# A deformable convolution on TensorE: strips of two rows in place of four, and more distance between the engines

## The chip, the cores and the metric

The kernel runs on one core of a Trainium2 chip. The metric is the device time of one execution in microseconds (us), taken as the median of three runs. Beside it stands one execution under the hardware profiler, which has a time of its own.

## The reference

Two layers in float32 on an image batch `x` of shape (2, 256, 128, 128), each a residual block that begins with a group norm over 32 groups (`_gn`). Layer 0 is a deformable 3x3 convolution: two plain 3x3 convolutions of the normalised input give, for each pixel and each of the 9 taps, an offset and a mask; the input is sampled bilinearly at the shifted place; the samples go through the weights.

```python
def _L0_conv_ref(x, w_conv, b_conv, w_off, b_off, w_mask, b_mask):
    offset = _conv2d(x, w_off, b_off)
    mask = jax.nn.sigmoid(_conv2d(x, w_mask, b_mask))
    ...
    py = base_y[None] + dy
    px = base_x[None] + dx
    sampled = jax.vmap(_deform_sample)(x, py, px)
    sampled = sampled * mask[:, None]
    out = jnp.einsum('bckhw,ock->bohw', sampled, w_conv.reshape(COUT, C, K2))
    return out + b_conv[None, :, None, None]
...
x = x + _L0_conv_ref(_gn(x), ...)
x = x + _L1_conv_ref(_gn(x), ...)
```

Layer 1 sends the normalised image through eight low-rank experts (a 1x3 convolution to 8 channels, a 3x1 convolution back to 256) and adds their outputs with the weights `probs`.

## The kernel before

**Stages.** At first (about 170 us) the kernel reads image 0, takes its statistics, and writes a table to DRAM: for every pixel one entry of 4 KB to be fetched, holding the four neighbours' 256 channels (four corners of 1 KB). Then comes the stream, which fills most of the time: all samples of image 0, then those of image 1. Beside image 0's samples the table of image 1 is built; beside image 1's samples layer 1 of image 0 runs. At the end (from about 3990 us) layer 1 of image 1 runs alone.

**A unit.** The stream's smallest step is a unit: one tap `k` of one image row `r`, that is 128 pixels, one to a partition. There are 2 x 128 x 9 = 2304 units. A unit passes through five engines:

- `gather` (L567, POOL): an indirect DMA fetches 128 entries of 4 KB into a tile `g`.
- `product` (L577, ACT): the first corner times its weight makes the accumulator `acc`.
- `add` (L583, DVE), three times: the other corners, times their weights, are added to `acc`.
- `turn` (L593, PE): two transposes of 128x128 put the sampled row, channels now on the partitions, into a PSUM tile `ptr` that takes two rows.
- `keep` (L601, ACT): each pair of rows is copied from `ptr` to an SBUF tile `sm`.
- `apply_tap` (L608, PE): the tap's weights times `sm`, accumulated over 9 taps and two halves of the input channels in a PSUM bank `po`.

After the ninth tap `residual` (L617, DVE) adds `po`, the bias and the old `x` into the tile of `x`, `result_stats` (L621) takes statistics for the next norm, and `store_x1` writes the rows out where they don't stay in SBUF.

**Chunks.** The order of units is: chunks of four rows (`CR`), in a chunk the nine taps, in a tap the four rows. So `sm` holds four rows (512 columns), and each of the four units of a tap issues one matmul of 512 columns: two output halves `m` times two input halves `h`. The halves `m` have a PSUM bank each, both used by every chunk.

**Order.** The instructions are issued in an order written out by hand, by a loop over slots `s`, one unit to a slot. Every engine works off its instructions in that order; semaphores keep the data dependencies. In slot `s` the loop issues the gather of unit `s + GA`, the product of `s + LP`, adds of `s + 1` and `s`, the tap of `s - LM`, the transposes of `s - TL`, and for every second unit the copy of `s - TL - KL`:

```python
if when(s + GA):
    gather(s + GA)
if when(s + LP):
    product(s + LP)
...
if when(s - TL):
    turn(s - TL)
if when(s - TL - KL) and (s - TL - KL) % 2 == 1:
    keep(s - TL - KL)
for piece in sched.pop(s, ()):
    piece()
```

All other work (offsets of the next group of rows, loads of `x`, the table of image 1, layer 1, residuals) hangs in `sched`, at slots given by `put`. How far one engine may run ahead of another follows from these distances and from the number of buffers: 15 tiles `g`, 8 `acc`, 3 `sm`, 3 `ptr`.

PSUM has eight banks: three for `ptr`, three (`p_m`) for all side work, two for `po`.

Of the kernel before, what the change touches and what calls it, by code (L numbers as in the profile page):

```python
# [32 lines left out]
F32 = mybir.dt.float32  # L33
# [6 lines left out]
P = 128  # L40
# [18 lines left out]
ER = 64  # L59
ROUND = 12582912.0  # L60

UPC = K2 * CR
UPG = UPC * CPG
UPI = UPG * NG
UNITS = B * UPI
GA = 15
LP = 3
TL = 1
KL = 2
LM = 8  # L70
XB, XR = 3, 5


@with_exitstack
def layers(ctx, tc, x, w_om, b_om, w_cv, b_cv, w_in, w_out, probs, out):
# [444 lines left out]


    gp = pool(stream, "gather", GA)
    ap = pool(stream, "acc", 8)
    sp = pool(stream, "sampled", 3)
    st = pool(stream, "stat", 1)
    p_o = pool(stream, "p_o", 1, space=PSUM)
    p_t = pool(stream, "p_t", 3, space=PSUM)
    oc = pool(stream, "offs", 1)
    pieces, _, last_rows = offset_pieces(0, oc, p_m, "m")
# [19 lines left out]

    def unit(u):  # L550
        b, u = divmod(u, UPI)
        ci, u = divmod(u, UPC)
        k, r = divmod(u, CR)
        return b, ci, k, r

    gts, accs, pts, sms, pos_, stats1 = {}, {}, {}, {}, {}, {}

    def sample_of(u):
        b, ci, k, r = unit(u)
        idx, wt = ready[b, ci // CPG]  # L560
        return idx, wt, (ci % CPG) * CR + r, k

    def gather(u):
        b, ci, k, r = unit(u)
        idx, _, rr, k = sample_of(u)
        gt = gp.tile([P, 2 * CELL], F32, tag="gt", name=f"g_{b}_{ci}_{k}_{r}")
        nc.gpsimd.indirect_dma_start(  # L567
            out=gt[:], out_offset=None, in_=tables[b][:, :],
            in_offset=bass.IndirectOffsetOnAxis(ap=idx[:, rr, k : k + 1], axis=0),
        )  # L570
        gts[u] = gt

    def product(u):
        b, ci, k, r = unit(u)
        _, wt, rr, k = sample_of(u)
        acc = ap.tile([P, C], F32, tag="acc", name=f"acc_{b}_{ci}_{k}_{r}")
        nc.scalar.activation(acc, gts[u][:, 0:C], AF.Copy, scale=wt[:, 0, rr, k : k + 1])  # L577
        accs[u] = acc

# [5 lines left out]
        )  # L585

    def turn(u):
        b, ci, k, r = unit(u)
        if r % 2 == 0:
            pts[u // 2] = p_t.tile([P, NH, 2 * W], F32, tag="t", name=f"ptr_{b}_{ci}_{k}_{r}")  # L590
        acc = accs.pop(u)
        for h in range(NH):
            nc.tensor.transpose(  # L593
                pts[u // 2][:, h, (r % 2) * W : (r % 2 + 1) * W], acc[:, h * P : (h + 1) * P], ident
            )

    def keep(u):
        b, ci, k, r = unit(u)
        if r == 1:
            sms[u // CR] = sp.tile([P, NH, N], F32, tag="sm", name=f"sm_{b}_{ci}_{k}")  # L600
        nc.scalar.copy(sms[u // CR][:, :, (r - 1) * W : (r + 1) * W], pts.pop(u // 2))  # L601

    def apply_tap(u):
        b, ci, k, i = unit(u)
        m, h = divmod(i, NH)
        if k == 0 and h == 0:
            pos_[b, ci, m] = p_o.tile([P, N], F32, tag=f"o{m}", name=f"po_{b}_{ci}_{m}")
        nc.tensor.matmul(  # L608
            pos_[b, ci, m], lhsT=wcv[:, h, k, m * P : (m + 1) * P], rhs=sms[u // CR][:, h],
            start=(k == 0 and h == 0), stop=(k == K2 - 1 and h == NH - 1),  # L610
        )

    def residual(b, ci, m):
        xt = xts[b, ci // CPG]
        at_ = (ci % CPG) * N
        v = xt[:, m, at_ : at_ + N]
        nc.vector.scalar_tensor_tensor(v, pos_.pop((b, ci, m)), bcv[:, m : m + 1], v, ALU.add, ALU.add)  # L617

    def result_stats(b, ci, m):
        at_ = (ci % CPG) * N  # L620
# [6 lines left out]
    def table_beside(b):  # L627
# [57 lines left out]
        for j in range(NCH):  # L685
            g, i = divmod(j, CPG)
            if g < NG - XR:
                put(slot, lambda j=j: load(j, "xs"))
            elif i == 0:

                slot = max(slot, UPG * (g - NG + XR + 1) + LM + 12)
# [222 lines left out]
    assert tabled < UPI - GA - 16  # L914
    put(UPI - 16, sides.close)
    put(UPI, lambda: result_stats_of(1))
    slot = UPI + LM + 10
# [18 lines left out]
    while s < end or any(t >= s for t in sched):  # L936
# [21 lines left out]
        if when(s - TL - KL) and (s - TL - KL) % 2 == 1:  # L958
# [69 lines left out]
```

## Time and profile before

| | us |
|---|---|
| median of 3 runs | 4062.48 |
| lowest, highest | 4056.1, 4065.21 |
| profiled execution: time | 4155.75 |
| profiled execution: span from first to last instruction | 4154.0 |

| engine | busy us | share of the span |
|---|---|---|
| PE, matmuls | 3497.9 | 84% |
| PE, weight loads | 1870.3 | 45% |
| DVE | 3442.1 | 83% |
| ACT | 1837.6 | 44% |
| POOL | 2335.4 | 56% |

The profiled execution is 93 us longer than the median of the runs, so sums made from the profile are made against 4155.75 us. A row of the profile names a source line, an engine, an operation, its tiles (out<-in), how often it came, its busy time and the mean of one; then the idle time of the engine just before these instructions, and what ended it. A wait names the waiting instruction, the one that ended the wait, the total, how often, and the longest; "remote" there means that the profile doesn't tell what ended it, "issue" that the engine waited for nothing that the profile shows. Matmuls are pipelined and their ends modelled, so a mean of one is longer than the distance from one to the next.

### The profile page before, as it was taken

The page shows a single profiled execution, that of the slowest core. Times are in us where ns is not written, and L with a number is a line of the kernel's source. Part 1 is how long each engine was busy: PE and PEld are TensorE (multiplying, and loading weights), DVE is VectorE, ACT ScalarE, POOL GpSimd, SP SyncE. Part 2 cuts the span into 40 slices and gives each one's busy share as a digit, 9 for nine tenths or more (in the row PEclk, how much of TensorE's full clock was granted, in tenths as well). Part 3 has the DMA queues.
Part 4 walks back from the last instruction along what each step waited for, and adds up shares of the span by engine and source line. Part 5 has one row for each costly group of instructions (what it writes and reads, how often), then busy time and mean ns, then how long its engine had stood idle before and what let it go on. Part 6 is the DMA issues. An engine that isn't in the chain of part 4 may idle for free.

```text
span 4154.0 us, 51837 instructions
## 1 busy us (share of the span) xinstructions
PE 3497.9 (84%) x14044; PEld 1870.3 (45%) x14044; DVE 3442.1 (83%) x8066; ACT 1837.6 (44%) x3883; POOL 2335.4 (56%) x2388
## 2 busy tenths in 40 slices
PE   3588888888878888888889888889988889888889
PEld 2443434444444444444444444444545445444444
DVE  6488988888888887889788888888888888888887
ACT  2244444445444554444444444444444444444432
POOL 0356666656665666656566555556656556555531
PEclk9699999999999999989999999999999999999999
DMA  9999999999999999999889999999999999988835
GB/s 360 358 358 370 356 371 346 342 335 366 372 372 378 389 394 387 376 361 369 315 329 349 333 344 345 334 350 340 363 339 356 331 349 354 351 320 327 327 118 193
DMA packets 419516, 1425.46 MB, mean 343 GB/s; under 512 B 41582, under 2 KB 45338, under 8 KB 419098
## 3 DMA queue, kind: packets, MB, share of 16 engines
q0 software_dynamic: 331776, 1208.11, 78.0%
q1 hardware_dynamic: 87450, 214.04, 13.6%
q8 instruction: 114, 1.87, 0.2%
q14 instruction: 176, 1.44, 0.1%
HBM read 1298.20 MB, written 123.78 MB: 342 GB/s over the span
## 4 chain that ended last, share of the span: by engine, by line
PE 42%; DVE 25%; DMA 12%; issue 11%; another core or an unknown queue 6%; ACT 3%; POOL 1%; POOLq 1%; SPq 0%; ACTq 0%; DVEq 0%
PE po L608 23%; DVE acc L583 19%; DMA g<-table,cidx 9%; PE ptr L593 7%; PE pu L335 3%; PE pe L832 2%; PE ph L766 2%; DMA table<-hpx 2%; ACT acc L577 1%; PE ph L811 1%; PE pe L847 1%; DVE stats L621 1%; POOL g L567 1%; DVE x L617 1%
## 5 line engine op out<-in xcount | busy, mean ns | idle before, releaser
L583 DVE SCALAR_TENSOR_TENSOR acc<-g,wt,acc 128x256 f32<-128x256 f32 x6912 | 2961.8, 480 | 466.3 <-ACT acc L577 325.7
L567 POOL DMA_INDIRECT g<-table,cidx x2304 | 2284.5, 992 | 1530.9 <-DVE acc L583 556.5
L608 PE MATMUL po<-sm,wcv 128*128 128x512 f32 x4608 | 2502.1, 625 | 301.5 <-ACT sm L601 130.8
L601 ACT COPY sm<-ptr 128x512 f32<-128x512 f32 x1152 | 672.7, 584 | 1933.6 <-PE ptr L593 1096.3
L593 PEld LDWEIGHTS ptr<-idp,acc 128*128 128x128 f32 x4608 | 626.4, 146 | 1622.3 <-issue 1075.9
L593 PE MATMUL ptr<-idp,acc 128*128 128x128 f32 x4608 | 935.2, 286 | 195.4 <-ACT sm L601 76.3
L577 ACT ACTIVATE acc<-g,wt 128x256 f32<-128x256 f32 x2304 | 1060.1, 506 | 43.2 <-DMA g<-table,cidx 29.7
L608 PEld LDWEIGHTS po<-sm,wcv 128*128 128x128 f32 x4608 | 753.4, 199 | 375.3 <-ACT sm L601 160.4
L335 PE MATMUL pu<-wus,x 128*128 128x81 f32 (+2 forms) x1448 | 270.1, 313 | 7.8 <-issue 6.7
L335 PEld LDWEIGHTS pu<-wus,x 128*128 128x128 f32 x1448 | 216.8, 200 | 10.3 <-issue 6.9
L617 DVE SCALAR_TENSOR_TENSOR x<-po,bcv,x 128x512 f32<-128x512 f32 x116 | 86.3, 744 | 59.6 <-PE ptr L593 21.8
L832 PE MATMUL pe<-h,wout 128*128 128x256 f32 (+1 forms) x384 | 127.2, 461 | 1.0 <-DVE xc L856 1.0
L766 PE MATMUL ph<-xcn,win 128*64 128x254 f32 (+1 forms) x768 | 98.1, 403 | 4.6 <-issue 4.6
L856 DVE TENSOR_TENSOR xc<-pe,xc 128x512 f32<-128x512 f32 x76 | 49.8, 683 | 44.3 <-PE pe L847 20.0
L350 PE MATMUL om<-u,idp 128*128 128x216 f32 x192 | 56.0, 375 | 33.1 <-ACT u L344 30.7
L832 PEld LDWEIGHTS pe<-h,wout 128*128 128x128 f32 x384 | 67.9, 193 | 33.7 <-issue 30.1
L621 DVE BATCH_NORM_STATS2 stats<-x 128x6 f32<-128x512 f32 x116 | 79.2, 683 | 0.1
L766 PEld LDWEIGHTS ph<-xcn,win 128*64 128x64 f32 x768 | 55.9, 145 | 37.6 <-issue 16.6
L847 PE MATMUL pe<-h,wout 64*128 64x128 f32 (+1 forms) x752 | 70.1, 322 | 1.3 <-issue 1.3
L504 DVE COPY hpx<-hpt 128x512 f32<-128x512 f32 x32 | 21.1, 687 | 57.2 <-DMA table<-hpx 47.0
L799 DVE TENSOR_TENSOR v<-xcn 128x512 f32<-128x512 f32 x96 | 65.9, 744 | 1.8 <-ACT xcn L786 1.8
L847 PEld LDWEIGHTS pe<-h,wout 64*128 64x128 f32 x752 | 52.1, 187 | 27.4 <-issue 18.8
(115 smaller groups left out, 1019.3 us busy)
## 6 DMA issues: line engine op xcount, KB each, us to landing
g<-table,cidx POOLq DMA_INDIRECT x2304
table<-tpx SPq DMA_DIRECT2D x32, 1024.0 KB
table<-hpx SPq DMA_DIRECT2D x15, 2048.0 KB
x<-in_x_dram SPq DMA_DIRECT2D x29, 1024.0 KB
out_dram<-xc SPq DMA_DIRECT2D x38, 512.0 KB
x<-x SPq DMA_DIRECT2D x16, 1024.0 KB
out_dram<-x SPq DMA_DIRECT2D x26, 512.0 KB
xs<-in_x_dram SPq DMA_DIRECT2D x22, 512.0 KB
```

The costliest lines, as they stand in the source:

```text
L335: nc.tensor.matmul(held["ps", j][:, lo:hi], lhsT=xt[:, h, r * W : (r + 1) * W], rhs=w[:, lo - i + 2 : hi - i + 2], start=(i == 2 and h == ...
L567: nc.gpsimd.indirect_dma_start(out=gt[:], out_offset=None, in_=tables[b][:, :], in_offset=bass.IndirectOffsetOnAxis(ap=idx[:, rr, k : k + ...
L577: nc.scalar.activation(acc, gts[u][:, 0:C], AF.Copy, scale=wt[:, 0, rr, k : k + 1])
L583: nc.vector.scalar_tensor_tensor(accs[u], gt[:, q * C : (q + 1) * C], wt[:, q, rr, k : k + 1], accs[u], ALU.mult, ALU.add)
L593: nc.tensor.transpose(pts[u // 2][:, h, (r % 2) * W : (r % 2 + 1) * W], acc[:, h * P : (h + 1) * P], ident)
L601: nc.scalar.copy(sms[u // CR][:, :, (r - 1) * W : (r + 1) * W], pts.pop(u // 2))
L608: nc.tensor.matmul(pos_[b, ci, m], lhsT=wcv[:, h, k, m * P : (m + 1) * P], rhs=sms[u // CR][:, h], start=(k == 0 and h == 0), stop=(k == K ...
L617: nc.vector.scalar_tensor_tensor(v, pos_.pop((b, ci, m)), bcv[:, m : m + 1], v, ALU.add, ALU.add)
L621: nc.vector.bn_stats(stats1[b][:, m, ci], xts[b, ci // CPG][:, m, at_ : at_ + N])
L766: nc.tensor.matmul(o[:, :, to], lhsT=win[:, h, tap], rhs=pairs[:, t, :, of], start=(q == 0), stop=(q == 5),)
L832: nc.tensor.matmul(ps[t][:, m], lhsT=wout[:, 2 * t, m * P : (m + 1) * P], rhs=hs[ci], start=(banks or m == 0), stop=False,)
L847: nc.tensor.matmul(ps[t][:, m, to], lhsT=wout[half, 1, m * P : (m + 1) * P], rhs=hs[c][half, of], start=False, stop=(banks or m == NH - 1) ...
```

## The change

- Chunks become strips of two rows (`SR`): in a strip the nine taps, in a tap two rows. `sm` holds two rows (256 columns) and has four buffers. Each of the two units of a tap issues two matmuls of 256 columns, for one output half `m` and both input halves `h`.
- Both output halves of a strip share one PSUM bank, and the pool of `po` has two buffers, which the strips use in turn. Only the strip's first matmul carries `start`.
- `residual` works on 256 columns, once for each half of each strip, and is issued `LR` = 6 slots after the strip's last tap (before: 2). `result_stats` is still taken once for four rows and half, two slots after the residual; the store follows.
- `LP`: the first product is issued 6 units ahead, not 3. `KL`: the copies stand 4 slots behind the transposes, not 2. There are 15 buffers `acc`, not 8.
- `GA`: 14 buffers for gathers, 14 units ahead, not 15.
- Loads of `x` for the next group are issued 52 slots ahead, not 54; two other due slots are written in terms of `LR`, the one for layer 1 of image 0 falling two slots later.

```diff
-UPC = K2 * CR
-UPG = UPC * CPG
+SR = 2
+SPC = CR // SR
+SPG = GR // SR
+UPS = K2 * SR
+UPG = UPS * SPG
...
-GA = 15
-LP = 3
+GA = 14
+LP = 6
 TL = 1
-KL = 2
+KL = 4
 LM = 8
+LR = 6
...
-    ap = pool(stream, "acc", 8)
-    sp = pool(stream, "sampled", 3)
+    ap = pool(stream, "acc", 15)
+    sp = pool(stream, "sampled", 4)
     st = pool(stream, "stat", 1)
-    p_o = pool(stream, "p_o", 1, space=PSUM)
+    p_o = pool(stream, "p_o", 2, space=PSUM)
...
     def keep(u):
-        b, ci, k, r = unit(u)
-        if r == 1:
-            sms[u // CR] = sp.tile([P, NH, N], F32, tag="sm", name=f"sm_{b}_{ci}_{k}")
-        nc.scalar.copy(sms[u // CR][:, :, (r - 1) * W : (r + 1) * W], pts.pop(u // 2))
+        b, si, k, _ = unit(u)
+        sms[u // SR] = sp.tile([P, NH, SR * W], F32, tag="sm", name=f"sm_{b}_{si}_{k}")
+        nc.scalar.copy(sms[u // SR], pts.pop(u // SR))
 
     def apply_tap(u):
-        b, ci, k, i = unit(u)
-        m, h = divmod(i, NH)
-        if k == 0 and h == 0:
-            pos_[b, ci, m] = p_o.tile([P, N], F32, tag=f"o{m}", name=f"po_{b}_{ci}_{m}")
-        nc.tensor.matmul(
-            pos_[b, ci, m], lhsT=wcv[:, h, k, m * P : (m + 1) * P], rhs=sms[u // CR][:, h],
-            start=(k == 0 and h == 0), stop=(k == K2 - 1 and h == NH - 1),
-        )
-
-    def residual(b, ci, m):
-        xt = xts[b, ci // CPG]
-        at_ = (ci % CPG) * N
-        v = xt[:, m, at_ : at_ + N]
-        nc.vector.scalar_tensor_tensor(v, pos_.pop((b, ci, m)), bcv[:, m : m + 1], v, ALU.add, ALU.add)
+        b, si, k, m = unit(u)
+        if k == 0 and m == 0:
+            pos_[b, si] = p_o.tile([P, NH, SR * W], F32, tag="o", name=f"po_{b}_{si}")
+        for h in range(NH):
+
+            nc.tensor.matmul(
+                pos_[b, si][:, m], lhsT=wcv[:, h, k, m * P : (m + 1) * P], rhs=sms[u // SR][:, h],
+                start=(k == 0 and m == 0 and h == 0),
+                stop=(k == K2 - 1 and m == NH - 1 and h == NH - 1),
+            )
+
+    def residual(b, si, m):
+        at_ = (si % SPG) * SR * W
+        v = xts[b, si // SPG][:, m, at_ : at_ + SR * W]
+        nc.vector.scalar_tensor_tensor(v, pos_[b, si][:, m], bcv[:, m : m + 1], v, ALU.add, ALU.add)
...
-            put(slot - 54, lambda b=b, g=g: load_x(b, g + 1))
+            put(slot - 52, lambda b=b, g=g: load_x(b, g + 1))
...
-            b, ci, k, i = unit(u)
-            if k == K2 - 1 and i % NH == NH - 1:
-                m = i // NH
-                put(s + 2, lambda b=b, ci=ci, m=m: residual(b, ci, m), True)
-                put(s + 3, lambda b=b, ci=ci, m=m: result_stats(b, ci, m), True)
-                if m == NH - 1 and ci % CPG == CPG - 1 and not stays(b, ci // CPG):
-                    put(s + 4, lambda b=b, g=ci // CPG: store_x1(b, g))
+            b, si, k, r = unit(u)
+            if k == K2 - 1 and r == SR - 1:
+                for m in range(NH):
+                    put(s + LR + m, lambda b=b, si=si, m=m: residual(b, si, m), True)
+                    if si % SPC == SPC - 1:
+                        put(s + LR + 2 + m, lambda b=b, ci=si // SPC, m=m: result_stats(b, ci, m), True)
+                if si % SPG == SPG - 1 and not stays(b, si // SPG):
+                    put(s + LR + 4, lambda b=b, g=si // SPG: store_x1(b, g))
```

The numbering functions (`unit`, `sample_of`, `gather`, `product`, `turn`) count strips (`si`) where they counted chunks (`ci`); what they issue for a unit is the same.

More of the change, by code (lines that the diff above doesn't have):

```diff
@@ L551, in unit @@
         b, u = divmod(u, UPI)
-        ci, u = divmod(u, UPC)
-        k, r = divmod(u, CR)
-        return b, ci, k, r
+        si, u = divmod(u, UPS)
+        k, r = divmod(u, SR)
+        return b, si, k, r
     gts, accs, pts, sms, pos_, stats1 = {}, {}, {}, {}, {}, {}
     def sample_of(u):
-        b, ci, k, r = unit(u)
-        idx, wt = ready[b, ci // CPG]
-        return idx, wt, (ci % CPG) * CR + r, k
+        b, si, k, r = unit(u)
+        idx, wt = ready[b, si // SPG]
+        return idx, wt, (si % SPG) * SR + r, k
     def gather(u):
-        b, ci, k, r = unit(u)
+        b, si, k, r = unit(u)
         idx, _, rr, k = sample_of(u)
-        gt = gp.tile([P, 2 * CELL], F32, tag="gt", name=f"g_{b}_{ci}_{k}_{r}")
+        gt = gp.tile([P, 2 * CELL], F32, tag="gt", name=f"g_{b}_{si}_{k}_{r}")
         nc.gpsimd.indirect_dma_start(
@@ L573, in product @@
     def product(u):
-        b, ci, k, r = unit(u)
+        b, si, k, r = unit(u)
         _, wt, rr, k = sample_of(u)
-        acc = ap.tile([P, C], F32, tag="acc", name=f"acc_{b}_{ci}_{k}_{r}")
+        acc = ap.tile([P, C], F32, tag="acc", name=f"acc_{b}_{si}_{k}_{r}")
         nc.scalar.activation(acc, gts[u][:, 0:C], AF.Copy, scale=wt[:, 0, rr, k : k + 1])
@@ L587, in turn @@
     def turn(u):
-        b, ci, k, r = unit(u)
-        if r % 2 == 0:
-            pts[u // 2] = p_t.tile([P, NH, 2 * W], F32, tag="t", name=f"ptr_{b}_{ci}_{k}_{r}")
+        b, si, k, r = unit(u)
+        if r == 0:
+            pts[u // SR] = p_t.tile([P, NH, SR * W], F32, tag="t", name=f"ptr_{b}_{si}_{k}")
         acc = accs.pop(u)
@@ L593, in turn @@
             nc.tensor.transpose(
-                pts[u // 2][:, h, (r % 2) * W : (r % 2 + 1) * W], acc[:, h * P : (h + 1) * P], ident
+                pts[u // SR][:, h, r * W : (r + 1) * W], acc[:, h * P : (h + 1) * P], ident
             )
     def keep(u):
-        b, ci, k, r = unit(u)
-        if r == 1:
-            sms[u // CR] = sp.tile([P, NH, N], F32, tag="sm", name=f"sm_{b}_{ci}_{k}")
-        nc.scalar.copy(sms[u // CR][:, :, (r - 1) * W : (r + 1) * W], pts.pop(u // 2))
+        b, si, k, _ = unit(u)
+        sms[u // SR] = sp.tile([P, NH, SR * W], F32, tag="sm", name=f"sm_{b}_{si}_{k}")
+        nc.scalar.copy(sms[u // SR], pts.pop(u // SR))
     def apply_tap(u):
-        b, ci, k, i = unit(u)
-        m, h = divmod(i, NH)
-        if k == 0 and h == 0:
-            pos_[b, ci, m] = p_o.tile([P, N], F32, tag=f"o{m}", name=f"po_{b}_{ci}_{m}")
-        nc.tensor.matmul(
-            pos_[b, ci, m], lhsT=wcv[:, h, k, m * P : (m + 1) * P], rhs=sms[u // CR][:, h],
-            start=(k == 0 and h == 0), stop=(k == K2 - 1 and h == NH - 1),
-        )
-    def residual(b, ci, m):
-        xt = xts[b, ci // CPG]
-        at_ = (ci % CPG) * N
-        v = xt[:, m, at_ : at_ + N]
-        nc.vector.scalar_tensor_tensor(v, pos_.pop((b, ci, m)), bcv[:, m : m + 1], v, ALU.add, ALU.add)
+        b, si, k, m = unit(u)
[11 more added lines that the diff above has]
+        nc.vector.scalar_tensor_tensor(v, pos_[b, si][:, m], bcv[:, m : m + 1], v, ALU.add, ALU.add)
     def result_stats(b, ci, m):
@@ L689, in table_beside @@
             elif i == 0:
-                slot = max(slot, UPG * (g - NG + XR + 1) + LM + 12)
+                slot = max(slot, UPG * (g - NG + XR + 1) + LM + LR + 6)
                 put(slot, lambda g=g: load_group(g, "xs"))
@@ L916, in layers @@
     put(UPI, lambda: result_stats_of(1))
-    slot = UPI + LM + 10
+    slot = UPI + LM + LR + 6
     norms1[0], pieces = norm_pieces(stats1[0], st, p_m, "m", "1_0")
@@ L948, in layers @@
             apply_tap(u)
-            b, ci, k, i = unit(u)
-            if k == K2 - 1 and i % NH == NH - 1:
-                m = i // NH
-                put(s + 2, lambda b=b, ci=ci, m=m: residual(b, ci, m), True)
-                put(s + 3, lambda b=b, ci=ci, m=m: result_stats(b, ci, m), True)
-                if m == NH - 1 and ci % CPG == CPG - 1 and not stays(b, ci // CPG):
-                    put(s + 4, lambda b=b, g=ci // CPG: store_x1(b, g))
+            b, si, k, r = unit(u)
+            if k == K2 - 1 and r == SR - 1:
[5 more added lines that the diff above has]
+                    put(s + LR + 4, lambda b=b, g=si // SPG: store_x1(b, g))
         if when(s - TL):
```

## The prediction

> **What bounds the kernel now.** I read the busy shares and queues of the page first, then stretches of the span, then the groups, the waits, and the timeline at one long wait.
>
> ```profile
> PE 3497.9 (84%) x14044; PEld 1870.3 (45%) x14044; DVE 3442.1 (83%) x8066; ACT 1837.6 (44%) x3883; POOL 2335.4 (56%) x2388
> ...
> q0 software_dynamic: 331776, 1208.11, 78.0%
> q1 hardware_dynamic: 87450, 214.04, 13.6%
> ```
>
> The queues add to 91.9% of sixteen DMA engines' span (with 0.3% of instruction fetch): 3818 us of transfers in 4154 us, more than any engine's busy time. Now the stretches (second number: length; after the engines: clock, DMA share, GB/s):
>
> ```profile
> 0.00:200.00 200.00, 85.52 (x406) 69.30 (x407) 103.35 (x199) 52.24 (x81) 39.09 (x62) 0.80 0.96 360
> ...
> 1000.00:2000.00 1000.00, 846.05 (x3195) 452.37 (x3193) 839.67 (x2021) 493.71 (x1050) 608.27 (x610) 0.93 0.99 376
> 2000.00:3000.00 1000.00, 880.56 (x3574) 470.93 (x3574) 840.55 (x2009) 451.39 (x983) 595.03 (x601) 0.96 0.92 340
> 3000.00:3900.00 900.00, 792.47 (x3316) 428.57 (x3314) 751.38 (x1782) 404.11 (x876) 529.88 (x537) 0.95 0.93 340
> 3900.00:4154.00 254.00, 228.29 (x1181) 116.90 (x1180) 201.18 (x381) 83.20 (x124) 77.77 (x90) 0.97 0.50 188
> ```
>
> The first half is at the DMA's limit (0.99), the second is not (0.92), and there nothing is full: DVE 84%, PE 88%. Some wait paces it:
>
> ```profile
> ACT sm L601 <- PE ptr L593: 1096.3, 610, 9.5
> ...
> ACT sm L601 <- remote: 570.6, 91, 14.0
> ...
> DVE acc L583 <- ACT acc L577: 325.7, 79, 13.5
> ...
> ACT acc L577 <- DMA g<-table,cidx: 29.7, 18, 17.8
> ```
>
> ACT hardly waits for a gather (29.7 us), so the DMA does not hold the arithmetic up; it stands still because the buffers are full when DVE stands still. DVE's largest wait is for ACT's first products: 79 times, 4.1 us each. One such place, ACT's timeline and then DVE's:
>
> ```profile
> 2693.80 0.91 ACT L577 ACTIVATE acc<-g,wt 128x256 f32<-128x256 f32 x2
> 2704.39 0.59 ACT L601 COPY sm<-ptr 128x512 f32<-128x512 f32 x1 [9.68 <-remote]
> ```
> ```profile
> 2689.68 10.07 DVE L583 SCALAR_TENSOR_TENSOR acc<-g,wt,acc 128x256 f32<-128x256 f32 x23
> 2705.79 0.48 DVE L583 SCALAR_TENSOR_TENSOR acc<-g,wt,acc 128x256 f32<-128x256 f32 x1 [6.04 <-ACT acc L577]
> ```
>
> ACT stood 9.68 us at a copy whose transposes signalled late; the products are behind that copy, and DVE ran dry for 6.04 us. The loop PE, ACT, DVE has too little slack for delays of this size.
>
> **The change, part by part.** A slot is one sampled row of one tap: from 200 to 3900 us the trace has 6715 of L583's adds, three a slot, so 3700/2238 = 1.65 us.
>
> *Slack (LP 3 to 6, KL 2 to 4, acc 8 to 15).* Before: in slot s the copy needs transposes of slot s-2; DVE's first add in slot s needs the product of ACT's slot s-2; DVE can be 4 slots ahead of PE's signals. After: 4 and 5 slots, 9 in all. The accumulators don't undo it: a product reuses the tile of a transpose 4 slots back before, 8 after. The cover grows by 5 x 1.65 = 8.3 us against waits of 4.1 us mean; nearly all 325.7 us on DVE can go. PE's taps still follow their copies by 2 slots; its transposes follow the copy that frees their bank by 1 slot instead of 3, which leaves that loop (5 slots round) as it was. PE's waits for ACT's copies (130.8 + 76.3 us in the list) therefore stay, or shrink a little.
>
> *Two banks and late residual (LR 6).* PE waited 90.0 us for L617 before a new group's first tap; the same bank now comes back a strip of 18 slots later, and the residual runs 11 slots before that: 0 left. DVE stood idle 59.6 + 9.9 us in front of L617 (its two forms), as it came two slots behind PE's last tap; with six, near 0. Late next is nothing: the statistics and the store that follow are on nobody's path.
>
> *Residuals doubled.* 128 of 512 columns become 256 of 256. Of 256 columns no row reads PSUM; the adds of 256 take 480 ns, the residual of 512 takes 744. So 256 x 0.48 - 128 x 0.744 = +28 us of DVE; least +0 if only columns counted, most +95 at full price each. I take 28, hidden in DVE's 16% idle; were DVE the limit, it would all show. The statistics stay 128.
>
> *Matmuls of 256 columns.* 4608 of 512 in the trace (two passes of each) become 9216 of 256, with 4608 weight loads more. The timeline holds both sizes under the same conditions:
>
> ```profile
> 2707.86 1.02 PE L608 MATMUL po<-sm,wcv 128*128 128x512 f32 x2
> ...
> 2710.57 1.03 PE L832 MATMUL pe<-h,wout 128*128 128x256 f32 x4
> ```
>
> Two of 512 take 1.02 us, four of 256 take 1.03, each with its own weight load of 190 ns hidden in about 215 ns of streaming. By this row the cost is 0. The groups give the other end: L832's 256 form has 67.8 us busy in 256 (265 ns), its 512 form 59.4 in 128 (464): 2 x 265 - 464 = 66 ns, x 4608 = 304 us. The Trainium skill speaks against the change here (Perfetto Trace Analysis, Matmuls): larger matmuls are more efficient than smaller, though the same paragraph wants independent groups to rotate through banks. By the rule PE pays something up to 304 us; by the row nothing. I take 0: back-to-back spacing sets PE's rate and the group's means hold idle starts. Cover: PE's idle 12%, about 0.2 us a slot.
>
> *Instruction fetch.* 9216 more PE instructions, 33% more; the fetch queue of PE moved 1.87 MB, so +0.6 MB, 2 us of transfer. Of the PE waits that nothing explains (70.0 + 51.3 us at L608 and L593) a third more would be 40 us; taken 0 to 40, 0 on the path.
>
> *Gathers (GA 15 to 14, product three slots earlier).* POOL issues the gather of unit s+14 after DVE's slot s, and ACT wants it in slot s+8; before s+15 and s+12. Counting 128 packets of 4 KB to each gather in the trace, landing comes 4.4 us after the issue in the median, 7.9 at 95%; then the data lies about 10 us until its product starts. Four slots (6.6 us) of this go, so some products will now wait. Behind a waiting product on ACT stand copies, and PE waits for those; DVE has five slots before it notices. Cost 0 to 20 us, 0 taken, cover being the 9-slot slack. Copies keep count and size (1152 of 512). Loads of x move by two slots on SP's queue (52 instead of 54 ahead), and 52 slots are still 86 us.
>
> *Sum.* DVE could gain 325.7 + 69.5 - 28 = 367 us, but the DMA allows less. Its idle in the stream, 200 to 3900 us: 0.05 x 800 (a stretch of 200 to 1000 reads 0.95) + 0.01 x 1000 + 0.08 x 1000 + 0.07 x 900 = 193 us. The best stretch stood at 0.99; with 0.98 over all, 74 us remain idle: gain 119 us, so 4155.75 - 119 = 4037 us under the profiler. The median, 4062.48, is 93 us below the profiled execution. With the same 3818 us of transfers it has 244 us of idle, of which 8 (first 200 us) and 127 (last 254) lie outside the stream: 109 left. In proportion 119/193 x 109 = 67 us: **3995 us**. The case's own range: 3955 (all 109 gone) to 4030 (half of the 67).
>
> The skill would forbid even this. DMA: Bandwidth & Descriptors (Where 436 GB/s comes from) puts a core's HBM at about 358 GB/s: 1425 MB need 3981 us, and with 135 us of idle at the ends 4116, above the median already. Here 1000 us ran at 376 GB/s and the page's slices reach 394, so the trace decides: the share of the engines is the cap I use.
>
> **The rivals.**
> 1. *The DMA was the limit all along outside the profiler, or the wait moves to the gathers.* For: the median is 93 us shorter with the same bytes; 0.99 in the first half; four slots less lead. Against: 29.7 us of gather waits now. Gain 0 to 20: 4042 to 4062.
> 2. *Slower: PE becomes the bound through weight loads.* Its place is the second half, where PE also serves the other layer and is 88% busy. Half of the 304 us, 152, fall there. PE's idle there, 12% of 1900 us, is waits that a slower PE need not shorten, so at worst the 152 show in full; with the waits' 67 still gained that is 4062 + 152 - 67 = 4147. It decides once a slot on PE costs 0.2 us more (its idle share of a slot), 50 ns for each of the four passes. Against: the 1.03 us row.
> 3. *Part only:* the residual's waits go (69.5 us of DVE), ACT's remain because PE's late signals grow with its instructions: about half of the gain, 4030.
>
> **How the numbers follow.** Main case 0.55 (3995), rival 3 0.14 (4030), rival 1 0.15 (4055), rival 2 0.16 (4147 at its full price). About 0.2%, 8 us, is what a measurement can tell. Faster: 0.55 + 0.14 + a small part of rival 1 = 0.71; same 0.12; slower 0.17. Range: 3945 (a little under all idle gone) to 4085 (half-way into rival 2, or 20 us of ACT on gathers over no gain).
>
> **What would show it.** Right: DVE waiting for ACT's products falls from 325.7 to under 60 us; L617 idle near 0; PE waiting for L617 gone; ACT waiting for gathers rises well above 29.7; DMA share 0.97 or more in 2000 to 3900. Tap matmuls spaced about 215 ns. Wrong: four taps taking over 1.2 us; PE busy 95% in the second half; DMA share still 0.92.

## The result, and the profile after

The change makes the kernel slower: 4205.01 us in the median (4185.29 to 4220.73) against 4059.45 us (now the median of four runs of the kernel before), a ratio of 1.0355 with the interval 1.0308 to 1.0401. The profiled execution took 4206.3 us, its span is 4204.6 us. The forecast was 3995 us, in a range of 3945 to 4085.

One caution for what follows: the profiled execution of the kernel before (4155.75 us) is 2.3% above the median of its runs, while in each of the other 19 traces shown here it is within 0.7% of it. So that page was probably taken under other conditions than those runs, perhaps on another chip; which one is not known. Where it matters, two traces from one chip stand below.

The page after: busy shares, PE's instruction fetch (q8) and the groups that matter:

```profile
PE 3589.1 (85%) x18652; PEld 2811.8 (67%) x18652; DVE 3445.2 (82%) x8194; ACT 1865.2 (44%) x3883; POOL 2316.9 (55%) x2388
...
q8 instruction: 150, 2.46, 0.2%
...
L587 DVE SCALAR_TENSOR_TENSOR acc<-g,wt,acc 128x256 f32<-128x256 f32 x6912 | 2952.5, 480 | 298.7 <-ACT acc L581 189.6
...
L612 PE MATMUL po<-sm,wcv 128*128 128x256 f32 x9216 | 2560.6, 397 | 203.6 <-issue 192.4
...
L621 DVE SCALAR_TENSOR_TENSOR x<-po,bcv,x 128x256 f32<-128x256 f32 x232 | 110.3, 476 | 84.3 <-remote 37.8
...
L368 DVE TENSOR_TENSOR pm<-om,at 128x216 f32<-128x216 f32 x28 | 10.7, 383 | 135.8 <-PE om L354 100.3
L860 DVE TENSOR_TENSOR xc<-pe,xc 128x512 f32<-128x512 f32 x76 | 49.9, 684 | 86.7 <-PE pe L851 80.1
```

The adds on the page before:

```profile
L583 DVE SCALAR_TENSOR_TENSOR acc<-g,wt,acc 128x256 f32<-128x256 f32 x6912 | 2961.8, 480 | 466.3 <-ACT acc L577 325.7
```

DVE's work is the same to within 4 us, and its adds wait less: 298.7 us stand before them, where 466.3 stood. But the idle time came back at other lines of DVE, all of which follow PE: the positions of the next group (L368; 15.8 us before), the sums of layer 1 (L860; 44.3 us before), the residual (L621; 59.6 us before). On PE the largest idle time of the taps no longer has a releaser: "issue". From the list of waits:

```profile
ACT acc L581 <- DMA g<-table,cidx: 390.1, 385, 18.2
...
PE po L612 <- issue: 192.4, 282, 2.4
...
PE ptr L597 <- issue: 108.1, 148, 5.8
DVE pm L368 <- PE om L354: 107.3, 20, 10.6
```

On the page before, PE's unexplained waits at these two lines were 70.0 and 51.3 us. Now the stretches of the second half (clock, DMA share and GB/s at the end of a line):

```profile
2000.00:3000.00 1000.00, 887.78 (x4706) 706.13 (x4705) 820.51 (x1989) 449.96 (x963) 577.03 (x589) 0.93 0.90 334
3000.00:3900.00 900.00, 798.24 (x4291) 632.50 (x4290) 733.07 (x1771) 399.30 (x848) 509.60 (x520) 0.93 0.89 330
```

The DMA share of the second half fell from 0.92 and 0.93 to 0.90 and 0.89, where the forecast had 0.97 or more. What "issue" looks like is seen in PE's timeline:

```profile
2705.77 1.07 PE L612 MATMUL po<-sm,wcv 128*128 128x256 f32 x4
...
2706.99 2.60 PE L770 MATMUL ph<-xcn,win 128*64 128x256 f32 x20
2710.58 0.59 PE L770 MATMUL ph<-xcn,win 128*64 128x254 f32 x2 [1.00 <-issue]
2712.02 0.59 PE L770 MATMUL ph<-xcn,win 128*64 128x254 f32 x2 [0.84 <-issue]
2712.76 1.13 PE L612 MATMUL po<-sm,wcv 128*128 128x256 f32 x4 [0.15 <-issue]
```

Four passes of taps take 1.07 us, near the 1.03 us that four passes of this size took before. Then PE, with no wait that the profile shows, starts one instruction (a weight load or a matmul, each of two passes) every 0.71 us for several microseconds: with the weight loads, which this view leaves out, at 2709.16, 2709.87, 2710.58, 2711.31, 2712.02 and 2712.75 us. Then it goes on as if nothing had been. I call at least three such steps in a row (0.60 to 0.78 us from start to start, starts within about 0.1 us of each other counted as one) a slow stretch. Counted in the traces: 8 of them, 20 us in sum, in the profiled execution before, and 73, 249 us, in that after.

### The profile page after: what moved, and what is told of

It is laid out like the page before. It is cut to its first block, busy times and chain, and to the rows that moved or that the text cites. A ratio compares the mean times of both kernels' runs of the same rounds, so it can differ in the third digit from the quotient of the medians.

```text
span 4204.6 us, 61411 instructions
## 1 busy us (share of the span) xinstructions
PE 3589.1 (85%) x18652; PEld 2811.8 (67%) x18652; DVE 3445.2 (82%) x8194; ACT 1865.2 (44%) x3883; POOL 2316.9 (55%) x2388
## 3 DMA queue, kind: packets, MB, share of 16 engines
q8 instruction: 150, 2.46, 0.2%
## 4 chain that ended last, share of the span: by engine, by line
PE 49%; DVE 23%; issue 14%; DMA 10%; another core or an unknown queue 2%; ACT 1%; SPq 1%; POOLq 0%; POOL 0%; DVEq 0%; ACTq 0%
PE po L612 29%; DVE acc L587 18%; PE ptr L597 8%; DMA g<-table,cidx 8%; PE pu L339 4%; PE ph L770 2%; PE pe L836 2%; DMA table<-hpx 2%; PE pe L851 1%; PE ph L815 1%; DVE stats L625 1%; DVE x L621 1%; PE om L354 1%; DVE tstats L655 1%
## 5 line engine op out<-in xcount | busy, mean ns | idle before, releaser
L587 DVE SCALAR_TENSOR_TENSOR acc<-g,wt,acc 128x256 f32<-128x256 f32 x6912 | 2952.5, 480 | 298.7 <-ACT acc L581 189.6
L612 PE MATMUL po<-sm,wcv 128*128 128x256 f32 x9216 | 2560.6, 397 | 203.6 <-issue 192.4
L612 PEld LDWEIGHTS po<-sm,wcv 128*128 128x128 f32 x9216 | 1669.3, 199 | 441.6 <-issue 302.7
L581 ACT ACTIVATE acc<-g,wt 128x256 f32<-128x256 f32 x2304 | 1098.2, 507 | 573.5 <-DMA g<-table,cidx 390.1
L597 PE MATMUL ptr<-idp,acc 128*128 128x128 f32 x4608 | 945.6, 285 | 206.6 <-issue 108.1
L597 PEld LDWEIGHTS ptr<-idp,acc 128*128 128x128 f32 x4608 | 642.6, 146 | 591.6 <-issue 241.5
L339 PE MATMUL pu<-wus,x 128*128 128x81 f32 (+2 forms) x1448 | 286.1, 321 | 41.4 <-issue 40.8
L621 DVE SCALAR_TENSOR_TENSOR x<-po,bcv,x 128x256 f32<-128x256 f32 x232 | 110.3, 476 | 84.3 <-remote 37.8
L770 PE MATMUL ph<-xcn,win 128*64 128x254 f32 (+1 forms) x768 | 116.9, 412 | 34.0 <-issue 33.0
L368 DVE TENSOR_TENSOR pm<-om,at 128x216 f32<-128x216 f32 x28 | 10.7, 383 | 135.8 <-PE om L354 100.3
L860 DVE TENSOR_TENSOR xc<-pe,xc 128x512 f32<-128x512 f32 x76 | 49.9, 684 | 86.7 <-PE pe L851 80.1
L681 ACT COPY tpx<-tpt 128x512 f32<-128x512 f32 x64 | 37.5, 586 | 124.1 <-PE ptr L597 57.8
L348 ACT COPY u<-pu 128x324 f32<-128x324 f32 x64 | 27.2, 426 | 111.4 <-PE ptr L597 38.0
```

The source lines that it names most:

```text
L339: nc.tensor.matmul(held["ps", j][:, lo:hi], lhsT=xt[:, h, r * W : (r + 1) * W], rhs=w[:, lo - i + 2 : hi - i + 2], start=(i == 2 and h == ...
L587: nc.vector.scalar_tensor_tensor(accs[u], gt[:, q * C : (q + 1) * C], wt[:, q, rr, k : k + 1], accs[u], ALU.mult, ALU.add)
L597: nc.tensor.transpose(pts[u // SR][:, h, r * W : (r + 1) * W], acc[:, h * P : (h + 1) * P], ident)
L612: nc.tensor.matmul(pos_[b, si][:, m], lhsT=wcv[:, h, k, m * P : (m + 1) * P], rhs=sms[u // SR][:, h], start=(k == 0 and m == 0 and h == 0) ...
L621: nc.vector.scalar_tensor_tensor(v, pos_[b, si][:, m], bcv[:, m : m + 1], v, ALU.add, ALU.add)
L770: nc.tensor.matmul(o[:, :, to], lhsT=win[:, h, tap], rhs=pairs[:, t, :, of], start=(q == 0), stop=(q == 5),)
```

## The experiments

**Chips.** The kernel before took 4060, 4138 and 4064 us on three occasions (the result, and the two chips called irregular below), and 3702 us on three other chips. On the first kind of chip, which I call irregular, PE has slow stretches in every trace; on the second, regular, not one in any. (No trace of the kernel before was taken on a regular chip. Each chip was met on one occasion only, so whether it is the chip or the occasion is not shown.) So a ratio is to the kernel before on the same chip, and the size of an effect is told for each kind.

The theories: A, the doubled tap instructions cost PE time; B, the shorter lead of the gathers holds up ACT; C, DVE now runs up to nine slots ahead of PE and then stops at side work that follows PE by two to four slots, so that the wait only moves.

| kernel | chip | us | ratio to before |
|---|---|---|---|
| after, as first measured | irregular | 4205.01 | 1.0355 [1.0308, 1.0401] |
| e1_slack: before, distances alone | irregular 1 | 4274.01 | 1.0324 [1.0289, 1.0359] |
| e2_strips: after without the distances | irregular 1 | 4181.27 | 1.0097 [1.0065, 1.0129] |
| e3_split: before, taps split | irregular 1 | 4199.59 | 1.0152 [1.0120, 1.0184] |
| e4_wide: after, one wide tap | irregular 1 | 4155.93 | 1.0051 [1.0028, 1.0074] |
| after_again | regular 1 | 3723.51 | 1.0057 [1.0040, 1.0074] |
| c2_nopm: after, no stop at positions | regular 1 | 3707.74 | 1.0015 [1.0008, 1.0021] |
| l6_products: before, products six ahead | regular 1 | 3713.48 | 1.0032 [1.0019, 1.0045] |
| k4_copies: before, copies four behind | regular 1 | 3711.16 | 1.0024 [1.0014, 1.0034] |
| before_again | irregular 2 | 4071.12 | 1.0005 [0.9989, 1.0022] |
| after_third | irregular 2 | 4223.02 | 1.0387 [1.0362, 1.0413] |
| c3_late_pos: after, positions follow PE by eight | irregular 2 | 4166.61 | 1.0258 [1.0234, 1.0282] |
| c2_again | irregular 2 | 4179.43 | 1.0275 [1.0247, 1.0303] |
| c4_wide_late_pos: c3 and e4 together | regular 2 | 3706.77 | 1.0014 [1.0005, 1.0023] |
| e4_again | regular 2 | 3720.16 | 1.0049 [1.0033, 1.0066] |
| l6_again | regular 2 | 3713.33 | 1.0029 [1.0017, 1.0041] |
| k4_again | regular 2 | 3711.41 | 1.0025 [1.0016, 1.0034] |
| c4_again | regular 3 | 3708.68 | 1.0016 [1.0009, 1.0023] |
| l6_third | regular 3 | 3713.80 | 1.0029 [1.0018, 1.0041] |

### The parts, on a first irregular chip

**The distances alone, on the kernel before** (e1_slack).

```diff
-GA = 15
-LP = 3
+GA = 14
+LP = 6
-KL = 2
-LM = 8
+KL = 4
+LM = 10
-    ap = pool(stream, "acc", 8)
+    ap = pool(stream, "acc", 12)
```

> The distances alone, with chunks of four rows and taps of 512 columns as before: first products six units ahead, copies four slots behind, 14 gathers, 12 accumulators; the tap moves from 8 to 10 slots behind, since it must come after the later copy. Theory A (the loss comes from the doubled number of PE instructions for the taps): the distances are harmless or good, 3990 to 4060 us. Theory B (the loss comes from the shorter lead of the gathers: products wait on their gathers, with the copies behind them): slower, 4130 to 4220 us, with gather waits of ACT in the hundreds of us as in the changed kernel (390.1).

**The change without the distances** (e2_strips).

```diff
-GA = 14
-LP = 6
-KL = 4
+GA = 15
+LP = 3
+KL = 2
-    ap = pool(stream, "acc", 15)
+    ap = pool(stream, "acc", 8)
```

> The changed kernel with the old distances: first products three ahead, copies two behind, 15 gathers, 8 accumulators. Strips of two rows, taps of 256 columns, two banks in turn and the late residual stay. Theory A (PE instructions): still slow, 4150 us or more, as the late signals of PE have less cover. Theory B (gather lead): back to 4060 us or below, ACT's waits on gathers under 60 us.

**Each tap of the kernel before split into two of 256 columns** (e3_split).

```diff
-        nc.tensor.matmul(pos_[b, ci, m], ...)
+        for c in range(2):
+            cols = slice(c * N // 2, (c + 1) * N // 2)
+            nc.tensor.matmul(pos_[b, ci, m][:, cols], ...)
```

> The kernel before with each tap matmul of 512 columns split into two of 256 columns with the same weights, so 9216 in place of 4608 matmuls and weight loads of L608; nothing else changes. Theory A: slower by 100 to 250 us, about 4160 to 4310, and stretches in the trace where PE issues one instruction each 0.7 us, as in the changed kernel. Theory B: 4060 us within 10, since the streamed columns are the same.

**The changed kernel with one tap of 512 columns for two of 256** (e4_wide). It leaves out part of the taps' sum, and PE streams as many columns as in the kernel after, in half the tap instructions.

```diff
-        for h in range(NH):
-            nc.tensor.matmul(pos_[b, si][:, m], lhsT=wcv[:, h, k, ...], rhs=sms[u // SR][:, h], ...)
+        nc.tensor.matmul(
+            pos_[b, si].rearrange("p h x -> p (h x)"), lhsT=wcv[:, m, k, 0:P],
+            rhs=sms[u // SR].rearrange("p h x -> p (h x)"), ...)
```

> The changed kernel with one tap matmul of 512 columns per unit in place of two of 256: the same streamed columns, half the matmuls and weight loads. It leaves out part of the sum: one weight block runs over both input halves side by side, which are then not added. Theory A: the loss is gone, 3980 to 4050 us, and the DMA share of the second half rises to 0.95 or more. Theory B: still about 4200 us, with gather waits of ACT near 390 us.

*What was measured.* No part is faster than before. Splitting the taps costs 1.5% by itself, though their spacing is the same (1.03 us for four passes); the wide tap stands at 0.5%, where the changed kernel lost some 3.6 to 3.9% (on other irregular chips). The distances cost 3.2% by themselves, and the change without them only 1.0%. So A holds on such a chip, but not alone. The waits of the distances alone:

```profile
ACT acc L577 <- DMA g<-table,cidx: 470.8, 423, 18.4
...
DVE acc L583 <- ACT acc L577: 192.4, 53, 8.7
...
DVE pm L364 <- PE om L350: 110.4, 26, 9.1
...
DVE x L617 <- PE po L608: 94.6, 24, 9.2
```

That is the picture of C: DVE stands at PE's offsets and PE's taps (no trace of the kernel before from this chip stands beside it). And those of the wide tap:

```profile
ACT acc L581 <- DMA g<-table,cidx: 432.1, 431, 18.5
...
DVE acc L587 <- ACT acc L581: 152.2, 44, 7.4
...
DVE pm L368 <- PE om L354: 110.0, 24, 8.0
```

ACT waits 432.1 us for gathers and the kernel stands 0.5% from before: B is not what costs. DVE stops 110.0 us at the positions as well, and yet there is no large loss. That PE, with half the tap instructions, still had idle time to make up a stop (idle behind ACT's copies, 200 to 3900 us: about 190 us here, 25 us in the kernel after) is my reading and not shown; the distances alone speak against it, with about 140 us of such idle time and a loss of 3.2%.

The slow stretches: 26 with the distances, 59 with the strips, 42 with split taps, 26 with the wide tap. So the two kernels with the distances have the same stop at the positions and as many slow stretches, and cost 3.2% and 0.5%: neither of the two explains the 3.2% by itself. The granted clock separates the parts in another way. The kernel before ran at 0.937 to 0.944 on this chip, the strips at 0.936 to 0.940 and the split taps at 0.938 to 0.939; but the distances alone ran at 0.914 to 0.919, and the wide tap, which has the distances too, at 0.924 to 0.930. On this chip, then, the slow stretches are many with doubled taps, and the lower clock comes with the distances. As an estimate from these figures, the clock withheld ((1 - clock) x time) is 105 us more with the distances than before, of 136 us of loss; but with the wide tap it is 55 us more, and the loss is 18, so it need not show in full. Why the distances lower the clock is not shown.

### A regular chip

**The kernel after, unchanged** (after_again).

> The changed kernel itself once more, on the chip of the three others, so that their ratios can be set against it. All theories: 2.5 to 3.6% slower than the kernel before.

**The kernel after with DVE's positions not taken from PE's offsets** (c2_nopm; the image's part of the offsets is left out).

```diff
-            nc.vector.tensor_tensor(t("pm", [P, GR, NO]), om, at, ALU.add)
+            nc.vector.tensor_tensor(t("pm", [P, GR, NO]), base, at, ALU.max)
```

> The changed kernel, with the sampling positions (L368) made from the constant part alone, so that this DVE instruction no longer waits for the offset matmuls of PE; the matmuls are still issued. It leaves out the image's part of the offsets. Theory C (DVE now runs so far ahead of PE that it stops at the side work that follows PE by two to four slots: positions, layer 1's sums): the 107 us of DVE's waits on om go and most of that comes off the time, 60 to 110 us faster than the changed kernel (1.5 to 2.6%). Theory B (shorter lead of the gathers): same as the changed kernel within 0.7%, the wait reappearing on ACT's products.

**The first products alone, and the copies alone, on the kernel before** (l6_products: LP 6, GA 14, 12 buffers `acc`; k4_copies: KL 4, LM 10).

> The kernel before with the first products six units ahead alone (12 accumulators, 14 gathers); copies two slots behind and taps eight as before. Theory B: most of the loss of both distances together (3.2%) is here, 2 to 3.5% slower, ACT waiting over 300 us for gathers. Theory C: DVE can be seven slots ahead of PE instead of four, so some of the loss, 0 to 1.5%, with DVE waiting for PE at the positions and residuals; ACT's gather waits cost nothing by themselves.

> The kernel before with the copies four slots behind the transposes alone, the taps therefore ten; products, gathers and accumulators as before. Theory B: no loss, since the lead of the gathers is the old one: within 0.7% of before, or faster. Theory C: DVE may be six slots ahead of PE instead of four: 0.5 to 1.5% slower, DVE's waits on ACT's products falling from 325 us to about 200 and its waits on PE rising by as much or more.

*What was measured.* Here the change costs 0.57%. The same program as in the result, on the page of this chip, and its stretch 2000 to 3000:

```profile
PE 3338.4 (90%) x18652; PEld 2669.1 (72%) x18652; DVE 3437.7 (92%) x8194; ACT 1957.2 (53%) x3883; POOL 2405.9 (65%) x2388
...
L612 PE MATMUL po<-sm,wcv 128*128 128x256 f32 x9216 | 2388.7, 382 | 0.0
```
```profile
2000.00:3000.00 1000.00, 971.79 (x5687) 800.43 (x5686) 963.38 (x2339) 556.30 (x1129) 703.21 (x691) 1.00 1.02 399
```

The taps have no idle time before them at all, the clock is 1.00, the DMA share 1.02: what the forecast wanted to reach, this chip has with the changed kernel, and by its time (3702 us) with the kernel before as well. ACT waits 1250.2 us for gathers in this run; how long it waits in the kernel before is not traced here, so B is bounded only by what is left of the loss. The positions' stop is 45.7 us here; without it the kernel gains 16 us of the 21 it had lost. That is C at its price on a regular chip: 0.42 of 0.57%. (c2_nopm also changes which entries are gathered, since its positions leave out the image; c3 and c4 below, which keep them, give nearly the same price.) Products alone and copies alone each cost 0.2 to 0.3%.

### A second irregular chip, with the trace of before beside

**The kernels before and after, unchanged** (before_again, after_third).

> The kernel before, unchanged, so that its trace stands beside the others of this call on the same chip. Every theory expects a ratio of 1.000 within 0.003 for it; a wider gap would say how little a small ratio is worth. What is read from it is whether the irregular stretches of TensorE (one instruction per 0.7 us) are few in it (8 in the first trace of before, 73 in that of after) on this chip as well.

> The changed kernel on the chip of this call. If the chip is one on which TensorE issues irregularly (the kernel before at 4060 us or more), 1.03 to 1.04; if it is one on which it does not (3702 us before), 1.005 to 1.006. A value between the two would say that it depends on more than the chip.

**The kernel after with the offsets on PE six slots earlier, copied out of PSUM by ACT, and the positions on DVE at their old slot** (c3_late_pos), so that they follow PE's product by about eight slots.

```diff
+        def s_keep():
+            nc.scalar.copy(t("omc", [P, GR, NO])..., held["om"][:, : GR * NO])
+
         def s_pos():
-            om = held["om"][:, : GR * NO].rearrange("p (r o) -> p r o", o=NO)
+            om = held["omc"]
...
-        pieces += [(55, s_pos), (56, s_mask)]
+        pieces += [(57, s_keep), (61, s_pos), (62, s_mask)]
...
-                put(slot - 68 - GA + n, piece, opens)
+                put(slot - 74 - GA + n, piece, opens)
```

> The changed kernel with the offsets of the next group worked out six slots earlier on TensorE, and their PSUM tile copied out by ScalarE, while VectorE's first side piece on them keeps its slot: it then stands about eight slots behind TensorE's last product of the offsets, and not two. If VectorE's stops at the side pieces cost the time (107 us in the first trace of after), its wait for that product goes to nearly nothing and the kernel gains 0.4% on a regular chip and up to 1.5% on an irregular one. If they are only the place where a late TensorE shows, the wait goes to other rows and the time stays within 0.3%.

**The positions not taken from the offsets, as on the regular chip** (c2_again).

> The changed kernel with the positions not taken from TensorE's product of the offsets at all (the image's part of the offsets is left out), so that VectorE never waits there. If those stops cost the time: at least as fast as the kernel with the positions moved, 0.4% below the changed kernel on a regular chip, up to 2.5% on an irregular one. If they only show it: within 0.3% of the changed kernel.

*What was measured.* The kernel before against itself is 1.0005. The loss is 3.9%. The waits of the two on this one chip, before_again and then after_third:

```profile
DVE acc L583 <- ACT acc L577: 271.5, 80, 7.1
...
PE po L608 <- issue: 111.9, 71, 7.1
...
PE ptr L593 <- issue: 37.0, 43, 6.0
```
```profile
DVE acc L587 <- ACT acc L581: 219.5, 69, 7.5
...
PE po L612 <- issue: 207.4, 277, 1.8
...
DVE pm L368 <- PE om L354: 107.3, 22, 9.6
PE ptr L597 <- issue: 107.2, 151, 1.9
```

DVE saves only 52 us at ACT's products. All idle time before its adds falls by 94 us (419.3 to 325.7), while that at the positions grows by 119 us (3.2 to 122.1), at layer 1's sums by 67 and at the residual by 40. Moving the positions takes away 1.3 points of the loss; not reading the product of the offsets at all takes no more. In the waits of c3_late_pos the stop at the positions is down to 21.8 us:

```profile
DVE acc L590 <- ACT acc L584: 240.5, 75, 9.7
...
PE po L615 <- issue: 208.7, 285, 2.3
...
DVE xc L863 <- PE pe L854: 89.6, 27, 7.7
...
DVE x L624 <- remote: 53.1, 13, 7.9
...
DVE pm L371 <- ACT omc L366: 21.8, 5, 6.9
```

What is left is mostly on PE. Counted in the four traces of this chip, 200 to 3900 us (idle: neither a matmul nor a weight load; which idle time has a releaser changes by some 25 us with the way of matching waits to weight loads):

| | before | after | c3_late_pos | c2_again |
|---|---|---|---|---|
| PE idle with no releaser, us | 138 | 352 | 352 | 369 |
| PE idle behind ACT, DVE or another, us | 310 | 76 | 55 | 41 |
| slow stretches in the whole span (us) | 7 (18) | 76 (253) | 78 (246) | 75 (257) |
| half-clock time, us | 345 | 625 | 632 | 672 |
| DVE idle, us | 492 | 624 | 571 | 584 |

The distances did what they were made for on PE: its waits for others fell from 310 to 76 us. But nearly as much idle time came back with no releaser. Over the span, 4070.0 to 4227.9 us, PE's matmuls are busy 128 us more (3477.9 to 3606.2). Of its half-clock time PE is busy in 83% before and 73% after, 286 and 456 us; the 170 us more at half speed make about 85 of the 128 us (an estimate). That PE is then the bound on this chip is how I read this; no run takes away the lower clock or the slow stretches of the full change, and with the positions moved both stay (0.909 to 0.912 against 0.911 to 0.915, 78 stretches), while the time falls by 1.3 points.

### Two more regular chips

**The wide tap and the moved positions together** (c4_wide_late_pos, c4_again), **the wide tap alone** (e4_again), **products and copies alone** (l6_again, k4_again, l6_third): the edits above.

> The changed kernel with the positions six slots further behind TensorE's offsets and, in place of two taps of 256 columns, one of 512 (part of the taps' sum is left out; TensorE streams as many columns in as many instructions as the kernel before). On an irregular chip: if the doubled instructions and the stop at the positions are the whole of the loss, they add: 1.0387 less 0.013 less 0.03 is 0.995, at or below the kernel before. If the distances cost by another way as well (TensorE's irregular issue grows with them), 1.005 to 1.015. On a regular chip 0.998 to 1.003.

> The changed kernel with one tap of 512 columns in place of two of 256, alone (part of the taps' sum is left out), as the base for the kernel with the positions moved as well. 1.005 as before, if this chip is irregular; about 1.003 if it is regular. If the stop at the positions costs the same with wide taps, it stands 1.3% above the kernel with both; if the stop is harmless once TensorE has fewer instructions, the two are within 0.3%.

> The kernel before with first products six units ahead, gathers 14 ahead and twelve accumulators, alone. On an irregular chip the two distances together cost 3.2%. If the cause is that VectorE runs ahead of TensorE and then stops at work that follows TensorE, this part alone (it adds three slots of lead of ScalarE over VectorE and none between TensorE and VectorE) costs little: 1.00 to 1.01. If the cause is the shorter lead of the gathers, most of the 3.2% is here. 1.003 on a regular chip.

> The kernel before with the copies four slots behind the transposes and the taps ten behind, alone. If the lead between TensorE's transposes and its taps is what costs, through residuals that VectorE meets before TensorE has done the taps, most of the 3.2% is here on an irregular chip: 1.02 to 1.03, with VectorE waiting at the residual for over 80 us. If only both distances together cost, 1.00 to 1.01. 1.002 on a regular chip.

> The changed kernel with the positions moved and one tap of 512 columns in place of two of 256 (part of the taps' sum is left out). On an irregular chip: 0.995 if the doubled instructions and the stop at the positions are the whole loss and add; 1.005 to 1.015 if the distances cost by another way too; TensorE's irregular stretches 20 to 30 in number in place of 76. On a regular chip 1.001.

> The kernel before with first products six units ahead, gathers 14 ahead and twelve accumulators. On an irregular chip: 1.00 to 1.01 if VectorE's lead over TensorE is what costs, up to 1.03 if the shorter lead of the gathers is; TensorE's irregular stretches stay near 7 if they come with the tap's form or with the copies' distance, and rise to some 25 if they come with this one. On a regular chip 1.003.

*What was measured.* All ran on regular chips, so they could not tell the parts on an irregular one apart. On regular chips they nearly close the sum: wide tap alone 1.0049 beside 1.0057 for the change, hence about 0.1% for the doubled instructions, which the intervals do not tell from nothing nor from 0.3%; with the positions moved as well 1.0014 and 1.0016, so the stop at the positions is worth 0.35%, near the 0.42% of c2_nopm. The 0.15% that remain bound what the shorter lead of the gathers can cost here. Products alone (1.0029) and copies alone (1.0025) came out as on the first regular chip. With the products alone the clock is lower here too (0.974 against 0.982 before), with the copies alone it is not (0.982). The copies show a wait that the change's second bank removes (PE at L608 for the residual, 70.1 us), the products one at the residual that still follows by two slots:

```profile
ACT acc L577 <- DMA g<-table,cidx: 1058.3, 1486, 18.4
...
DVE x L617 <- PE po L608: 40.2, 29, 3.6
```

No kernel here beats the one before on either kind of chip. Of the versions that compute everything and keep both parts of the change, c3_late_pos is 1.2% faster than the change on an irregular chip (1.0258 against 1.0387) and still 2.6% behind the kernel before; the strips without the distances are 1.0% behind.

## Why the prediction was wrong

- **The bound.** Read rightly: the DMA was not the limit of the second half, and something paced it. (Nor was 0.99 of the first half a ceiling: on a regular chip the share was 1.02, at 399 GB/s.) The 9.68 us at a copy "whose transposes signalled late" was read rightly as well: in the trace those transposes end at 2697.19 us, and the signal that let the copy go came at 2704.37. Read wrongly: that slack against such delays would shorten the time. Meanwhile PE did not stand; from 2690 to 2703.5 us it streamed matmuls with no gap above 0.2 us. Distance between engines covers a late signal, but it adds nothing to what PE gets done.
- **Slack: "nearly all 325.7 us on DVE can go", "late next is nothing".** This is the step that failed first. 189.6 us remained, where under 60 was the sign (on one chip, 271.5 fell to 219.5). And what the adds gained, 94 us on that chip, moved and grew: 119 us more at the positions, 67 at layer 1's sums, 40 at the residual. I had listed only the residual as a place where DVE follows PE, and had overlooked the positions (two slots behind PE) and the sums. c2 and c3 give the stop at the positions its price: 1.1 to 1.3 points of 3.9 on an irregular chip; on a regular one c2 and c4 give 0.35 to 0.42 of 0.57.
- **Two banks and late residual.** PE's wait for L617 went from 90.0 us to nothing, as said. L621 near 0 was wrong: 84.3 us on the irregular chip, 3.7 on a regular one (after_again), so six slots are enough only where PE is on time.
- **Doubled residuals.** 232 of 476 ns for 116 of 744: +24 us in the shown form, 28 forecast, and not on the path.
- **Matmuls of 256 columns, taken at 0.** The spacing was right, and on regular chips the 0 nearly so (about 0.1%, not told from nothing). On an irregular chip the split alone costs 1.5%. "PE's idle 12%" was no sure cover: of 448 us of PE's idle time before, 138 had no releaser, and after it was 352 of 428. The Trainium skill's rule (Perfetto Trace Analysis, Matmuls), which I had set aside because four and two took the same time back to back, was right for this chip in sign, by a way that the page does not speak of.
- **Instruction fetch.** The bytes came out (1.87 to 2.46 MB). The term beside it was the one mis-sized in the sum: for PE's waits that nothing explains I had 40 us more at most and none on the path. At the two lines I named they went from 121.3 to 300.5 us (192.4 + 108.1), and on one chip from 148.9 to 314.6. They are not shown to come from the fetch.
- **Gathers.** ACT's waits rose as said, 29.7 to 390.1 us, and no loss on an irregular chip is seen to come from them.
- **The sum.** 119 us of DVE's idle were to go; on the chip with both traces 131 us came (492 to 624). Scaling to the median by the two executions' idle time took the slowness of the profiled one for removable, although it may be that of another chip.
- **The rivals.** The first fits the regular chips, where the DMA share is 1.02 and nothing was gained. The second named slower, by way of PE, and came nearest (4147 us, measured 4205), but its mechanism, more than 50 ns for a pass, did not occur, and its place was half right: of the 158 us between the two traces of one chip, 56 are lost by the middle of the samples and 101 after it. So its nearness is in part luck. The third's reason, "PE's late signals grow with its instructions", did not occur as worded (the copies that start over 2 us after their transposes' end were 177 before and 148 after); what grew were the slow stretches.

What stays open is the larger part of the loss on an irregular chip: why PE issues at 0.71 us an instruction there, why the distances lower the clock, and which of the two costs what. In after_third none of the 76 stretches begins in a third of a group's 72 units, and 10 to 20 us ahead of one PE's matmuls were 93% busy against 87% in the mean, so a limit on sustained activity would fit; nothing here shows one. Whether the products or the copies carry the 3.2% of e1_slack, and whether the wide tap with the positions moved would beat the kernel before, was not seen on an irregular chip.

## What to carry to other kernels

Before you add distance between two engines, list every instruction of the engine that will run ahead which follows the other one, side work too, and move all of them, or the wait only changes its line. Idle time of an engine is sure cover for more instructions only if something releases it; a wait that you take away may come back as "issue" idle, as about 214 of PE's 234 us did here. Take a ratio on the chip where both kernels ran, and on more than one: the same edit cost 0.6% on one chip and 3.9% on another.

## What the runs showed of the hardware

- The same program, the kernel before, took 3702 us on three chips and 4064 to 4138 us on two others. In the kernel after, PE's idle time with no releaser was under 10 us on a regular chip and about 350 on an irregular one, the granted clock 0.984 and 0.911, the mean time of a gather's 4 KB packet 166 and 174 ns.
- On irregular chips PE's signals can arrive late while PE works on. In before_again ACT stood over 1 us ahead of 601 copies, and 177 of these started more than 2 us after the recorded end of their transposes, with 918 us of idle time on ACT; in after_third 148 of 287, with 786 us. In after_again, on a regular chip, it was 10 copies, none more than 0.1 us late. In the example at 2704 us (the profile of the kernel before) five signals for the transposes of five units, which end 1.1 to 2.3 us apart, arrive within 0.3 us. (The ends of matmuls are modelled in the profile.) Whether this and the slow stretches have one cause is not shown.
- Half clock without long idle times: between 200 and 3900 us after_third has 75 half-clock windows (625 us), and not one gap of over 3 us between matmuls. The Trainium skill (TensorE: Matmul & The Clock Gate, HAM oscillation) puts such windows down to idle gaps above some 3.4 us; by that section's rule there should be none here. And before_again, with 30 gaps of over 3.4 us, has less half-clock time (345 us). In after_third 45 of the 75 begin within 14 us after a slow stretch, and 31% of all moments lie so; but the strips, with 59 stretches, ran at the clock of the kernel before, so the stretches alone do not bring the lower clock.
- On a regular chip one core moved 399 GB/s over 1000 us.
